# Two copies of F, not one, ahead of the layernorm's last step in layer 0 of a two-layer graph attention kernel

## The chip, the cores and the metric

The kernel runs on one core of one Trainium2 chip. The metric is the time of one execution on the device in microseconds (us); lower is better. A core has five engines that run their own instruction queues side by side and wait for each other by semaphores: TensorE (PE in the profile), VectorE (DVE), ScalarE (ACT), GpSimd (POOL) and SyncE (SP). In this kernel POOL issues the gathers and scatters and SP the plain transfers.

## The reference, cut to what matters

Two graph attention layers run on 2708 nodes with 1024 features. The adjacency matrix is sparse and symmetric with a full diagonal; a node has about 17 neighbours.

```python
def _layernorm(x, axis=-1, eps=1e-5):
    m = jnp.mean(x, axis=axis, keepdims=True)
    v = jnp.var(x, axis=axis, keepdims=True)
    return (x - m) / jnp.sqrt(v + eps)

# layer 0
f = x @ Wf + bf
g = x @ Wg + bg
e = jax.nn.relu(f @ g.T)
scores = jnp.where(adj > 0, e, NEG)
attention = jax.nn.softmax(scores, axis=1)
x = _layernorm(x + attention @ (x @ W + bW))

# layer 1
h = x @ W
e = leaky_relu(h @ a1 + (h @ a2).T)
attention = softmax(where(adj > 0, e, NEG), axis=1)
x = _layernorm(x + relu(attention @ h))
```

## The kernel before, in words

A prelude turns the adjacency matrix into a list of neighbours for each node and folds Wf and Wg into one matrix M, so that the score of a node and a neighbour is a dot product of the node's row of F = x M with the neighbour's row of x (plus terms that depend on one of the two alone). The nodes are sorted by their number of neighbours and cut into 22 blocks of 128 (one has 32).

A block of 128 nodes has four groups of 32. A group's 32 nodes stand four times in the 128 partitions, so that one gathered tile of 128 rows holds four neighbours of each of the 32 nodes. A block has some 15 to 20 such tiles. They lie in `ring`, a buffer of 20 tiles in SBUF.

For a group, the 32 rows of F that belong to it have to stand four times below each other, too. That is what `replicate` does: four copies by ScalarE of 32 x 1024 numbers each, from the PSUM tile of F (`pm`) into an SBUF tile `Fr`. There are four `Fr` buffers, one for each group of a block. The scores are then made by `dots`: for each gathered tile one VectorE instruction multiplies the tile with its group's `Fr` and sums along the row (tile `j` is the product nobody reads). The tiles are taken in the order group 0, group 1, group 0, group 1 and so on, and then groups 2 and 3 in the same way.

The loop of layer 0 (line 1242) is a pipeline over blocks. Iteration k does, by engine:

- **VectorE**: the residual sum `z` and the layernorm's statistics of block k-1 (`close` and `norm`; the last of its small steps is `sh`), the query product of a later block (`q_dot`, `j<-xb,rb`), two products of the finished z with vectors that layer 1 needs (`j<-z,u2b` and `j<-z,u1b`), a reciprocal, the score products of block k+1 (`dots`), and their softmax (`soft`), which ends with `st`, the weights as TensorE wants them.
- **ScalarE**: copies of transposed y, group 0 of F of block k+1, the layernorm's last step (`z<-z,sh,rstd`, which waits for `sh` from VectorE), groups 1 and 2 of F, the scaling of block k's result (`y<-po,ri`), two copies of transposed x, group 3 of F, and later the exponential of the softmax.
- **TensorE**: the weighted sums of block k (`po<-ring,st`, which need `st`), transposes of x of block k+2, the product with W for block k-1, the product with M for block k+2 (the next F), transposes of y of block k.
- **GpSimd**: the gathers of block k+1's tiles, each as soon as the sums of block k have freed its place in the ring, then the scatter of z into layer 1's table (`T<-z`), and the loads of x, of the residual z and of later lists.
- **SyncE**: the write of z to memory (`X1S<-z`), behind the layernorm's last step.

Each engine keeps the order in which the program is written: the class `InOrder` (its line 71 is the line that the profile shows for every instruction of these layers, so instructions are told apart by their tiles). `close` is a generator: its first `next` runs the sum and the statistics up to `sh`, the second the layernorm's last step on ScalarE and SyncE's write, the third the two products on z, and what is left the scatter. So the place of a `replicate` between the `next(closing)` lines is its place in ScalarE's queue.

Of the kernel before, what the change touches and what calls it, by code (L numbers as in the profile page):

```python
# [106 lines left out]
def listed_path(ctx, tc, x, adj, Wf, bf, Wg, bg, W, bW, W1, a1, a2, out):  # L107
# [96 lines left out]
    def u_rows():  # L204

        for v, u in enumerate((u1b, u2b)):
            for h in range(H):
                pt = ps_t.tile([P, 4, P], F32, name="pt")
                for c in range(4):
                    k = 4 * h + c  # L210
                    pe.matmul(pt[:, c, :], uc[:, v, k:k + 1].to_broadcast([P, P]), ident, start=True, stop=True)
                act.copy(u[:, h * 512:(h + 1) * 512], pt.rearrange("p c i -> p (c i)"))
# [506 lines left out]
    def turn(rows, n, dst, halves=False):  # L719


        pts = []
        for k0 in range(0, KC, 4):
            pt = ps_t.tile([P, 4, P], F32, name="pt")
            at = slice(64, 64 + n) if halves and k0 and n < P else slice(0, n)
            for k in range(4):
                pe.transpose(pt[:, k, :n], rows[at, (k0 + k) * P:(k0 + k + 1) * P], ident[at, at])
            pts.append(pt)
        yield
        for k0, pt in zip(range(0, KC, 4), pts):  # L730
            if halves and k0 and n == P:
                for a, b in ((0, 64), (64, 0)):
                    act.copy(dst[:, k0:k0 + 4, a:a + 64], pt[:, :, b:b + 64])
            else:
                act.copy(dst[:, k0:k0 + 4, :n], pt[:, :, :n])

    def product(n, xT, w, row=None):


        pm = ps_m.tile([P, H, 512], F32, name="pm")  # L740
        for h in range(H):
            bias_row(pm, h, n, row)
        for h in range(H):
            half_product(pm, h, n, xT, w, row)
        return pm
# [20 lines left out]
    def split_product(xT, w, parts, row=None, pm=None):  # L766

        pm = ps_m.tile([P, H, 512], F32, name="pm") if pm is None else pm  # L770
        for h in range(H):
            c = slice(h * 512, (h + 1) * 512)
            if row is not None:
                pe.matmul(pm[:32, h, :], pick[:, row:row + 1].to_broadcast([P, 32]), rows3[:, c], start=True, stop=False)
            for k in range(KC // Q):
                for p in range(Q):
                    i = p * KC // Q + k
                    pe.matmul(pm[32 * p:32 * p + 32, h, :], xT[:, i, :32], w[:, i, c],
                              start=(k == 0 and (row is None or p > 0)), stop=(k + 1 == KC // Q))
        yield  # L780
        act.copy(parts, flat(pm))
        yield
        pm = ps_m.tile([P, H, 512], F32, name="pm")
        for h in range(H):
            pe.matmul(pm[:, h, :], rep, parts[:, h * 512:(h + 1) * 512], start=True, stop=True)
        return pm

    def whole(steps):

        while True:  # L790
            try:
                next(steps)
            except StopIteration as end:
                return end.value
# [261 lines left out]
    def load_lists(b):  # L1056
        for g in groups[b]:
            gather(pool, SL[:, g, :], LD[:, :], idq[:, g:g + 1], N * Q)
# [9 lines left out]
    with s0s:  # L1068
# [9 lines left out]
        def load_x(b):  # L1078
            xb[b] = xp.tile([P, D], F32, name="xb") if b > 0 else zs[:, :D]
            gather(pool, xb[b][:nrows[b]], x, ids[:nrows[b], b:b + 1])  # L1080
# [5 lines left out]
        def q_dot(b):  # L1086
            n = nrows[b]
            qs = small.tile([P, 1], F32, name="qs")
            dot(xb[b][:n], rb, n, qs[:n])
            qd[b] = spread(qs[:n], n, "qd")  # L1090

        def q_spread(b):
            n = nrows[b]
            pt = ps_t.tile([P, 4, P], F32, name="pt")
            pe.matmul(pt[:, 0, :Q], rep[:n], qd.pop(b)[:n], start=True, stop=True)
            yield
            q[b] = small.tile([P, Q], F32, name="q")
            dve.tensor_scalar(q[b], pt[:, 0, :Q], s0, None, op0=ALU.add)

        def x_turn(b):  # L1100
            xTs[b] = tp.tile([P, KC, P], F32, name="xT")
            for _ in turn(xb[b], nrows[b], xTs[b]):
                pass

        def f_product(b):
            F[b] = product(nrows[b], xTs.pop(b), M, 0)

        def replicate(b, k):

            Fr[b, k] = frp.tile([P, D], F32, name="Fr")  # L1110
            for p in range(Q):
                act.copy(Fr[b, k][32 * p:32 * p + 32, :], flat(F[b])[32 * k:32 * k + 32, :])

        def dots(u, lo, hi):
            for m in range(lo, hi):
                k, g, t = u.tiles[m]
                dot(lay.rows(u.at + m), Fr[u.b, k], P, u.sc[:, k, t:t + 1])
# [6 lines left out]
        def load_residual(b):  # L1124

            t, at = lay.slots[(lay.next + b + 2 - NB) % lay.count]
            Z[b] = zs if b + 2 < NB else t[:, at, :]
            gather(pool, Z[b][:nrows[b], :D], x, ids[:nrows[b], b:b + 1])
# [113 lines left out]
        for k, u in enumerate(units):  # L1242
            nxt = units[k + 1] if k + 1 < len(units) else None
            b = u.b
            back = seq[k - 1] if k > 0 else None
            ahead = seq[k + 2] if k + 2 < NB else None

            first = k == 0
            po = ps_s.tile([P, H, 512], F32, name="po")
            y[b] = yp.tile([P, D], F32, name="y")  # L1250
            if back is not None:
                for _ in yTs[back][1]:
                    pass
            reps = list(range(len(nxt.gs))) if nxt is not None and not first else []
            for r in reps[:1]:
                replicate(nxt.b, r)
            next(closing, None)
            if loaded is not None:
                q_dot(loaded)
                loaded = None  # L1260
            next(closing, None)
            for r in reps[1:3]:
                replicate(nxt.b, r)
            if nxt is None:

                for _ in closing:
                    pass
                Wp[back] = product(P, yTs.pop(back)[0], Wt, 1)
            lay.sums(u, po, y[b])
            if first:  # L1270
                u_rows()
            for _ in closing:
                pass
            closing = iter(())
            if ahead is not None and not first:
                x_turn(ahead)
            if k + 3 < NB and not first:
                loaded = seq[k + 3]
                load_x(loaded)
            if back is not None and nxt is not None:  # L1280
                load_residual(back)
                if back > 0:
                    Wp[back] = product(P, yTs.pop(back)[0], Wt, 1)
                else:
                    Wp[back] = whole(split_product(yTs.pop(back)[0], Wt, frp.tile([P, D], F32, name="Fr"), 1))
            if k + 2 == NB:
                load_residual(b)
            spreading = iter(())
            if ahead is not None and not first:
                spreading = q_spread(ahead)  # L1290
                next(spreading)
            for r in reps[3:]:
                replicate(nxt.b, r)
            if ahead is not None and not first:
                f_product(ahead)
            if ahead == NB - 1:
                sp.dma_start(M, W1.rearrange("(k p) d -> p k d", p=P))
            yT = tp.tile([P, KC, P], F32, name="xT")
            steps = turn(y[b], nrows[b], yT, halves=True)
            next(steps)  # L1300
            yTs[b] = yT, steps
            if k + 2 == NB:
                for _ in steps:
                    pass
            if k + 4 < NB and not first:
                load_lists(seq[k + 4])
            if nxt is not None:
                dots(nxt, 0, len(nxt.tiles))
            for _ in spreading:
                pass  # L1310
            if nxt is not None:
                soft(nxt)
            if back is not None:
                closing = close(back)
                next(closing)
# [529 lines left out]
```

## Time and profile before

| | us |
|---|---|
| median of 3 runs | 1885.37 |
| lowest and highest of them | 1868.06, 1900.10 |
| the profiled execution's own time | 1889.49 |
| its span, first to last instruction | 1887.8 |

| engine | busy us in the span | share | busy us from 507 to 1020 us |
|---|---|---|---|
| PE | 1614.6 | 86% | 489.55 |
| DVE | 1279.9 | 68% | 442.15 |
| ACT | 637.6 | 34% | 248.53 |
| POOL | 1180.3 | 63% | 362.23 |

The stretch from 507 to 1020 us holds twelve blocks of layer 0's loop. The mean of one 32 x 1024 copy of F is close to 1.0 us, that of one score product 1.23 us.

The profile is that of one execution. A row of groups gives busy time and the mean of one instruction, a row of waits gives the engine, the tile that it was about to write, what ended the wait, then the total in us, how often, and the longest. In a timeline the bracket is the engine's idle time ahead of the instruction and what ended it; "issue" means that the profile shows nothing that it waited for. Where a wait has several causes, the last by the profile is named.

### The profile page before, as it was taken

How to read it: one execution, taken by the hardware profiler on the slowest of the kernel's cores; microseconds unless marked ns; L12 is line 12 of the kernel's file. 1: busy time of each engine (PE TensorE's matmuls, PEld its weight loads, DVE VectorE, ACT ScalarE, POOL GpSimd, SP SyncE). 2: the span in 40 equal slices, each digit the busy share in tenths (PEclk: the TensorE clock that was granted, in tenths of full speed). 3: DMA queues.
4: the chain of work that ended last, by engine and by line, in shares of the span. 5: the costliest groups of instructions: out<-in, count | busy, mean ns of one | idle time of the engine just before them, and what ended most of it. 6: DMA issues, size and time to landing. Idle time of an engine off the chain costs nothing. (4 is left out here: it accounts for less than half of the span.)

```text
span 1887.8 us, 22782 instructions
## 1 busy us (share of the span) xinstructions
PE 1614.6 (86%) x6873; PEld 684.2 (36%) x6873; DVE 1279.9 (68%) x4158; ACT 637.6 (34%) x886; POOL 1180.3 (63%) x1130
## 2 busy tenths in 40 slices
PE   3898759788999999999999998279898988989896
PEld 2443324333443444444444443023333333323332
DVE  5996648767888888888888767246445445545543
ACT  5571425434554544444555551011111111111111
POOL 8892673555676777766767631666666666666630
PEclk7999889888999999999999999589999999989998
DMA  9671583656787778887777863999989999999950
GB/s 365 227 284 50 193 293 116 223 176 238 284 278 270 277 251 274 280 281 262 262 257 263 310 239 136 342 329 320 321 319 348 351 347 317 343 333 352 341 190 35
DMA packets 150961, 503.95 MB, mean 267 GB/s; under 512 B 32714, under 2 KB 32730, under 8 KB 148398
## 3 DMA queue, kind: packets, MB, share of 16 engines
q0 software_dynamic: 131648, 428.27, 63.9%
q1 hardware_dynamic: 16128, 73.71, 10.5%
q8 instruction: 56, 0.92, 0.2%
q10 hardware_dynamic: 3054, 0.43, 0.1%
q14 instruction: 75, 0.61, 0.1%
HBM read 510.81 MB, written 33.75 MB: 288 GB/s over the span
## 5 line engine op out<-in xcount | busy, mean ns | idle before, releaser
L71 POOL DMA_INDIRECT ring<-in_x_dram,SL x405 | 447.2, 1104 | 210.7 <-issue 95.1
L71 DVE SCALAR_TENSOR_TENSOR j<-ring,Fr 128x1024 bf16<-128x1024 f32 x402 | 493.1, 1227 | 100.3 <-ACT Fr L71 41.9
L71 PE MATMUL po<-ring,st 128*32 128x512 f32 x2616 | 376.9, 629 | 109.9 <-issue 56.2
L71 ACT COPY Fr<-pm 32x1024 f32<-32x1024 f32 (+2 forms) x353 | 340.6, 965 | 15.1 <-remote 6.5
L71 POOL DMA_INDIRECT ring<-T,SL x249 | 246.9, 992 | 122.9 <-issue 64.5
L71 PE MATMUL pm<-M,yT 128*128 128x512 f32 (+1 forms) x704 | 318.2, 601 | 4.5 <-issue 3.0
L71 PE MATMUL pm<-Wt,xT 128*128 128x512 f32 (+1 forms) x704 | 305.8, 603 | 12.2 <-issue 12.2
L71 PE MATMUL pm<-M,xT 128*128 128x512 f32 x672 | 298.5, 603 | 2.4 <-issue 2.4
L71 PEld LDWEIGHTS po<-ring,st 128*32 128x32 f32 x2616 | 109.4, 115 | 322.3 <-issue 258.6
L71 POOL DMA_INDIRECT more<-T,SL x156 | 155.0, 993 | 76.9 <-issue 42.8
L71 PEld LDWEIGHTS pm<-M,yT 128*128 128x128 f32 (+1 forms) x704 | 127.7, 187 | 195.7 <-issue 192.9
L71 PEld LDWEIGHTS pm<-Wt,xT 128*128 128x128 f32 (+1 forms) x704 | 131.2, 189 | 175.0 <-issue 171.1
L71 ACT ACTIVATE scores<-scores 128x12 f32<-128x12 f32 (+9 forms) x65 | 14.0, 216 | 520.2 <-DVE scores L71 415.2
L71 PEld LDWEIGHTS pm<-M,xT 128*128 128x128 f32 x672 | 130.5, 194 | 160.9 <-issue 158.2
L71 POOL TENSOR_TENSOR adj<-adj,iota 128x2708 f32<-128x2708 f32 (+2 forms) x23 | 124.5, 5446 | 17.0 <-ACT adj L71 17.0
L71 ACT ACTIVATE y<-po,ri 128x512 f32<-128x512 f32 (+1 forms) x88 | 58.1, 684 | 211.7 <-remote 134.4
L71 PE MATMUL pm<-halfT,Wt 128*128 128x512 f32 x256 | 114.3, 602 | 0.0
L71 POOL DMA_INDIRECT SL<-LD,idq x85 | 88.4, 1040 | 28.4 <-issue 25.8
L71 PE MATMUL po<-more,st 128*32 128x512 f32 x624 | 94.0, 659 | 13.2 <-issue 13.1
L71 DVE MAX8 cand<-adj 128x8 f32<-128x170 f32 x336 | 95.9, 325 | 12.4 <-POOL adj L71 12.4
L71 ACT COPY xT<-pt 128x512 f32<-128x512 f32 (+2 forms) x109 | 47.9, 499 | 85.6 <-PE pt L71 56.7
L71 POOL DMA_INDIRECT z<-in_x_dram,ids x21 | 25.1, 1194 | 81.3 <-DVE j L71 26.3
(236 smaller groups left out, 1436.0 us busy)
## 6 DMA issues: line engine op xcount, KB each, us to landing
adj<-in_adj_dram SPq DMA_DIRECT2D x19, 1354.0 KB
X1S<-z SPq DMA_DIRECT2D x19, 512.0 KB
ring<-in_x_dram,SL POOLq DMA_INDIRECT x405
rows<-in_L_gnn_Wg_dram SPq DMA_DIRECT2D x8, 512.0 KB
rows<-in_L_gnn_Wf_dram SPq DMA_DIRECT2D x8, 512.0 KB
M<-in_L_gnn_W_dram SPq DMA_DIRECT2D x1, 4096.0 KB
ring<-T,SL POOLq DMA_INDIRECT x249
u1b<-X1S SPq DMA_DIRECT2D x7, 512.0 KB
```

The source lines that it names most:

```text
L71: made = self.tc.keep_in_program_order(op(*args, **kwargs))
```

## The change

In each iteration of layer 0's loop, ScalarE's copies of group 1 of the next block's F move ahead of the layernorm's last step of the block before. Group 0 stands there already; group 2 stays behind it, and group 3 stays where it is. No instruction is added or taken away.

```diff
@@ -1252,14 +1252,14 @@
                 for _ in yTs[back][1]:
                     pass
             reps = list(range(len(nxt.gs))) if nxt is not None and not first else []
-            for r in reps[:1]:
+            for r in reps[:2]:
                 replicate(nxt.b, r)
             next(closing, None)
             if loaded is not None:
                 q_dot(loaded)
                 loaded = None
             next(closing, None)
-            for r in reps[1:3]:
+            for r in reps[2:3]:
                 replicate(nxt.b, r)
             if nxt is None:
```

## The prediction

> **What bounds the kernel now.** I began with the page's slices, because the change touches layer 0 alone and a share over the whole span says nothing of it.
>
> ```profile
> PE   3898759788999999999999998279898988989896
> DVE  5996648767888888888888767246445445545543
> ACT  5571425434554544444555551011111111111111
> PEclk7999889888999999999999999589999999989998
> ```
>
> A slice is 1887.8 / 40 = 47.2 us. Layer 0's loop runs from about 300 to 1150 us, slices 7 to 24. There TensorE (PE) is near full, from slice 10 on at its full clock, VectorE (DVE) at eight tenths and ScalarE (ACT) at four to five tenths. ACT has room; the question is whom its order keeps waiting. Next I asked who waits for whom in a stretch of twelve like blocks, 507 to 1020 us (43 us each), first for DVE (three of its rows), then for ACT, then for PE:
>
> ```profile
> DVE j L71 <- DMA ring<-in_x_dram,SL: 27.3, 49, 1.8
> DVE j L71 <- issue: 6.4, 13, 2.0
> ...
> DVE j L71 <- ACT Fr L71: 2.4, 8, 0.3
> ```
>
> ```profile
> ACT z L71 <- DVE sh L71: 32.4, 12, 5.6
> ```
>
> ```profile
> PE po L71 <- DVE st L71: 14.3, 11, 2.5
> PE po L71 <- issue: 7.6, 16, 0.8
> ```
>
> So PE waits for DVE's softmax weights (st) in eleven of twelve blocks, 1.3 us each: here a block ends when DVE ends. But DVE itself waits in its score products (j), some 3 us a block, mostly until a gathered row has landed in the ring. ACT, ahead of z, waits for DVE's sh.
>
> Third, the timeline of one block, ACT first. Columns are start, duration, instruction, number; the bracket is the idle time before it:
>
> ```profile
> 856.19 4.04 ACT L71 COPY Fr<-pm 32x1024 f32<-32x1024 f32 x4
> 862.34 1.24 ACT L71 ACTIVATE z<-z,sh,rstd 128x1024 f32<-128x1024 f32 x1 [2.11 <-DVE sh L71]
> 863.61 8.13 ACT L71 COPY Fr<-pm 32x1024 f32<-32x1024 f32 x8
> 871.76 1.27 ACT L71 ACTIVATE y<-po,ri 128x512 f32<-128x512 f32 x2
> ```
>
> One group of F is copied, ACT idles 2.11 us until the layernorm's shift is there, scales z, and copies two groups in one run. The same block on DVE:
>
> ```profile
> 862.09 0.22 DVE L71 TENSOR_SCALAR sh<-mv,rstd 128x1 f32<-128x1 f32 x1
> 862.21 1.22 DVE L71 SCALAR_TENSOR_TENSOR j<-xb,rb 128x1024 bf16<-128x1024 f32 x1
> ...
> 863.61 1.23 DVE L71 SCALAR_TENSOR_TENSOR j<-z,u2b 128x1024 bf16<-128x1024 f32 x1
> ...
> 866.15 1.23 DVE L71 SCALAR_TENSOR_TENSOR j<-ring,Fr 128x1024 bf16<-128x1024 f32 x1
> ...
> 867.69 1.23 DVE L71 SCALAR_TENSOR_TENSOR j<-ring,Fr 128x1024 bf16<-128x1024 f32 x1 [0.30 <-issue]
> ...
> 869.67 1.23 DVE L71 SCALAR_TENSOR_TENSOR j<-ring,Fr 128x1024 bf16<-128x1024 f32 x1 [0.75 <-DMA ring<-in_x_dram,SL]
> ...
> 889.51 1.23 DVE L71 SCALAR_TENSOR_TENSOR j<-ring,Fr 128x1024 bf16<-128x1024 f32 x1 [0.59 <-DMA ring<-in_x_dram,SL]
> ```
>
> The query product (j from xb) hides ACT's 1.24 us on z exactly: z's first product starts at 863.61 without a wait. Two products on z follow, then the score products; the second needs the second F group, and ACT's run delivers that at 863.61 + 4.06 = 867.67: DVE waits 0.30. That 0.30 is the price of today's order, and it is in nearly every block. Later score products wait for rows, the last at 889.51.
>
> **The change, part by part.** Nothing is added or removed. In 19 blocks (z starting between 321 and 1119 us) four 32x1024 copies, 4.06 us, pass ahead of z's scaling on ACT; the other engines' orders and POOL's and SP's issue orders stay as they are.
>
> *z's scaling, later.* ACT has the second group's F and a free Fr buffer (its last reader is the softmaxed block before), so the copies fill ACT's idle time and z starts 4.06 minus that idle later: 4.06 - 2.11 = 1.95 us in the block above. Behind z on DVE stand its two products (1.23 each), the reciprocal, and all score products: DVE idles those 1.95 us, from 863.6 to 865.55.
>
> *Second F group, earlier.* It is ready before the first score product, so the 0.30 goes. Net 1.65 us late from the second score product on.
>
> *What is late next.* Each later score product starts when its row has landed or when DVE is free. The rows' gathers follow PE's sums on POOL, started by the previous st, not by these products; I take the landings as fixed. A product that waited now waits that much less, and the delay shrinks by each wait. In this block the waits after the second product add to 0.75 + 0.48 + 0.40 + 0.19 + 0.31 + 0.29 + 0.59 = 3.0 us, more than 1.65: st stays where it is. The same replay in every block (ACT's idle before z; delay of z; DVE's waits over 0.12 us after the second product; what is left at st):
>
> | z starts (us) | idle | delay | waits | left |
> |---|---|---|---|---|
> | 321, 371, 423 | 0 | 4.06 | 4.1, 7.4, 7.9 | 0 |
> | 472 | 0 | 4.06 | 1.46 | 2.29 |
> | 515, 557, 646, 690, 733, 776 | 2.94, 2.08, 2.53, 2.95, 2.29, 2.82 | 1.1 to 2.0 | 3.2, 3.3, 3.0, 3.3, 3.2, 2.4 | 0 |
> | 604 | 5.6 | 0 | 2.4 | 0 |
> | 819, 862, 905, 948, 990 | 2.03, 2.11, 2.92, 2.04, 2.07 | 1.1 to 2.0 | 4.0, 3.0, 3.2, 2.5, 2.4 | 0 |
> | 1032 | 2.09 | 1.97 | 1.16 | 0.51 |
> | 1074 | 2.56 | 1.50 | 7.6 | 0 |
> | 1119 | 0 | 4.06 | 1.26 | 2.50 |
>
> The last 0.51 and 2.50 are hidden: PE takes up those blocks' st 3.5 us and more after it is made (st at 1062.5 and 1146.3, PE's sums at 1066.9 and 1150.7). The 2.29 at 472 is not: PE waited 0.17 us for that st. **Sum: +2.3 us.** If the cover were gone everywhere, see the first rival.
>
> *ACT's later work.* With its idle filled, ACT ends the third group, the scaling of y and the fourth group up to 2 us sooner. Nobody waits: PE runs from the x transposes at 867.28 to the end of the F product at 896.8 without a gap, and y's transposes stand behind that. I cost it at nothing; at most it gives the idle filled, 31 us over thirteen blocks.
>
> *SP's write of z and POOL's scatter.* The write is issued right behind z's scaling, 2 us later, and first reports come 2.5 us on; the scatter of z stands behind the block's gathers on POOL (888.60 here), 20 us later. Nothing.
>
> [...]
>
> **The total.** Profiled execution: span 1887.8 plus 1.7 around it = 1889.5; after, 1891.8. That execution is 4.1 us above the median of the three runs, 1885.4, so I give 1885.4 + 2.3 = **1888 us**.
>
> **Rivals.**
>
> *Slower: the delay reaches the matmuls.* Price: 5 blocks x 4.06 + 13 x 4.06 - 31.4 (idle of those thirteen) - 18 x 0.30 = 36.2 us; 1925.7 against the profile, 1921.6 against the median, +1.9%. For it: DVE releases PE in most blocks, and the margin is thin in some (1.7 against 2.4 at 990). Against it: the rows' landings are what DVE last waits for, and the three early blocks and 1074 have over 7 us or PE behind them. It decides once a block's waits for rows are below z's delay less 0.30, about 1.7 us, or if rows land later along with the products. Half exposed is 1904.
>
> *Faster: the copies are what counts.* DVE loses 18 x 0.30 = 5.4 us and nothing is given back: 1880 by the median. If ACT's gained idle also shortened blocks, 31 us: 1854. For it: ACT's idle is real. Against: z is waited for first by the same DVE, and PE's floor without any wait in the twelve blocks is (14.3 + 7.6) / 12 = 1.8 us a block below today, so 31 is out of reach.
>
> *No change at all*, because the order isn't what the diff says, is excluded: in the compiled order ACT's z stands behind four more copies in 19 blocks.
>
> **How the numbers follow.** Forecast 0.74, slower rival 0.17, faster rival 0.09. The three runs lie 17 us below to 15 above their median, and about 2% (38 us) is what a measurement tells from no change. The range goes from the faster rival's 1880 less half that spread, 1872, to the full exposure, 1921. Over 2% slower needs more than the full price, or that and a slow draw: half of that rival, rounded up, 0.10; over 2% faster has no mechanism, 0.03; within 0.87.
>
> **What would show it.** ACT's wait for sh ahead of z gone; the products on z waiting for ACT z about 1 to 2 us in each block of 507 to 1020; the 0.30 for the second F group gone; DVE's waits for rows down by some 1.5 us a block; PE's waits for st about as before (14 us) and blocks of 43 us. Wrong would be: waits for rows as large as before with longer blocks (the slower rival: landings move with DVE), or blocks shorter with PE waiting less for st.

## The result and the profile after

| | before | changed |
|---|---|---|
| median of 6 runs, us | 1888.92 | 1942.16 |
| lowest to highest | 1868.06 to 1900.10 | 1929.21 to 1952.61 |
| profiled execution, its span | 1889.49, 1887.8 | 1946.41, 1944.7 |

The ratio is 1.0295, 95% interval 1.0258 to 1.0331: slower, 53 us, where the forecast had 1888 and the range ended at 1921.

The page's slices of the changed kernel (those of before stand in the prediction):

```profile
PE   3896858898988898989999889359988888988876
DVE  5996648787878786868888667336445464544533
ACT  5571443544343444444445354001111111111111
PEclk8998879898989899989999899679989999989988
```

Every layer-0 engine is less busy, and PE's clock is no longer full in the middle. The loop, from the first to the last scaling of z, took 832.5 us before and 876.9 now: 44 of the 57 us that the spans differ by. Of the rest, 5 us lie ahead of the first of these scalings, 4.06 of them the copies that now stand in front of it, and 7 us behind the last, where no instruction was moved.

The waits of 507 to 1020 us, first DVE (its rows on `j`), then PE (all its rows on `pt`, and the one between them):

```profile
DVE j L71 <- issue: 51.3, 9, 8.9
DVE j L71 <- ACT Fr L71: 22.0, 3, 9.6
DVE j L71 <- ACT z L71: 11.0, 3, 4.6
```

```profile
PE pt L71 <- DVE ri L71: 16.5, 5, 3.3
PE pm L71 <- issue: 14.7, 14, 2.2
PE pt L71 <- issue: 13.2, 4, 3.3
PE pt L71 <- DVE j L71: 6.7, 2, 3.4
```

Two rows of before are gone: DVE waits for no row of the ring any more (27.3 us), and PE does not wait for st (14.3 us). In their place DVE waits for z, eleven times and 59 us in all (the row `ACT z` and 48 us of the first row, by the timeline), and PE waits eleven times, 3.3 us each, before it writes a tile `pt`. That tile is the one that PE's transposes go to. The profile names DVE's reciprocal `ri` for five of these waits, the product beside it for two and nothing for four; in time each ends as the one below does, with the reciprocal. One block of the changed kernel, ACT, DVE and PE in turn:

```profile
931.90 1.14 ACT L71 COPY xT<-pt 128x512 f32<-128x512 f32 x3 [2.84 <-PE pt L71]
932.91 8.12 ACT L71 COPY Fr<-pm 32x1024 f32<-32x1024 f32 x8
941.06 1.24 ACT L71 ACTIVATE z<-z,sh,rstd 128x1024 f32<-128x1024 f32 x1
942.33 4.06 ACT L71 COPY Fr<-pm 32x1024 f32<-32x1024 f32 x4
```

```profile
942.34 1.23 DVE L71 SCALAR_TENSOR_TENSOR j<-z,u2b 128x1024 bf16<-128x1024 f32 x1 [5.18 <-issue]
943.60 1.23 DVE L71 SCALAR_TENSOR_TENSOR j<-z,u1b 128x1024 bf16<-128x1024 f32 x1
...
944.75 0.17 DVE L71 RECIPROCAL ri<-pt 128x2 f32<-128x2 f32 x1
```

```profile
941.03 0.66 PE L71 MATMUL pt<-ident,xb 128*128 128x128 f32 x4
944.97 0.66 PE L71 MATMUL pt<-ident,xb 128*128 128x128 f32 x4 [3.29 <-DVE j L71]
...
945.90 15.59 PE L71 MATMUL pm<-Wt,xT 128*128 128x512 f32 x32
...
961.90 13.89 PE L71 MATMUL pm<-M,xT 128*128 128x512 f32 x32
975.63 1.04 PE L71 MATMUL pt<-ident,y 128*128 128x128 f32 x8
```

The same places on PE and DVE in the kernel before:

```profile
867.28 1.10 PE L71 MATMUL pt<-ident,xb 128*128 128x128 f32 x8
...
868.65 13.90 PE L71 MATMUL pm<-Wt,xT 128*128 128x512 f32 x32
```

```profile
866.03 0.17 DVE L71 RECIPROCAL ri<-pt 128x2 f32<-128x2 f32 x1
```

There are two `pt` buffers. In `sums` PE writes the softmax's totals into one, and only the reciprocal frees it. The second half of the x transposes needs that buffer. Before, the reciprocal was done at 866.20 us and the second half due at 867.7: some 1.5 us to spare. In the changed kernel the late z holds z's two products, they hold the reciprocal, and PE stands still in the middle of its transposes.

That closes a ring of waits, with its own length, in this block and the next: x transposes and the two products of PE 30.66 us (944.97 to 975.63), to the copies of y's transposes 0.69, two of those 1.01, eight copies of F 8.15, z's scaling 1.27, two products and the reciprocal 2.59, back to PE 0.05: **44.42 us**. In the list of z's starts eight of the nineteen intervals are 44.4 us and one 44.2, seven are 48 to 53, and ACT has no idle time ahead of z in any but the last. One more thing is in it: the product with W takes 15.59 us, not 13.90. The trace's windows of the kernel, with the granted clock as the third number from the end, show why:

```profile
946.00:949.40 3.40, 3.40 (x6) 1.32 (x5) 3.30 (x7) 3.35 (x6) 2.79 (x3) 0.50 1.02 406
949.40:990.00 40.60, 37.31 (x177) 16.20 (x177) 33.55 (x77) 17.02 (x21) 24.40 (x25) 1.00 0.73 249
```

The hole ends at 944.97 us; from 946.00 to 949.40 us PE is granted half its clock (0.50), then 1.00, and the product with W takes 1.7 us more than the 13.90 us of before.

The seven long intervals are not explained by this. The kernel before has three such, 49 to 52 us, all before 475 us. In all of them but the first of either kernel ACT stands still for 2 to 8 us at a time ahead of y's scaling or the copies of transposed x, and the profile names no instruction of this core that it waits for ("remote" or "issue"). So here, at 843 to 897 us of the changed kernel:

```profile
853.59 1.27 ACT L71 ACTIVATE y<-po,ri 128x512 f32<-128x512 f32 x2 [5.00 <-issue]
...
866.28 0.59 ACT L71 COPY xT<-pt 128x512 f32<-128x512 f32 x1 [7.12 <-remote]
```

In the same six of the seven PE, too, pauses 1.0 to 2.2 us at a time within or behind the product with W, and a second stretch at 0.50 of the clock, of 3.4 to 10.2 us, goes with them. By the intervals, the nine of 44.2 to 44.4 us are 1.4 us each over the 43.0 of before, some 13 of the 44 us; most of the rest stands in the four long intervals more. So on this chip the ring is shown, but what it is worth there is not.

### The profile page after: what moved, and what is told of

Its sections match the earlier page's. It is cut to its first block, busy times and chain, and to the rows that moved or that the text cites. A ratio compares the mean times of both kernels' runs of the same rounds, so it can differ in the third digit from the quotient of the medians.

```text
span 1944.7 us, 22760 instructions
## 1 busy us (share of the span) xinstructions
PE 1616.7 (83%) x6851; PEld 682.5 (35%) x6873; DVE 1281.3 (66%) x4158; ACT 638.6 (33%) x886; POOL 1151.4 (59%) x1130
## 5 line engine op out<-in xcount | busy, mean ns | idle before, releaser
L71 POOL DMA_INDIRECT ring<-in_x_dram,SL x405 | 418.0, 1032 | 276.9 <-issue 82.2
L71 PE MATMUL po<-ring,st 128*32 128x512 f32 x2616 | 342.5, 619 | 85.7 <-issue 34.1
L71 PE MATMUL pm<-Wt,xT 128*128 128x512 f32 (+1 forms) x704 | 333.1, 645 | 18.7 <-issue 18.5
L71 PEld LDWEIGHTS pm<-Wt,xT 128*128 128x128 f32 (+1 forms) x704 | 141.5, 204 | 198.2 <-issue 194.3
L71 PEld LDWEIGHTS po<-ring,st 128*32 128x32 f32 x2616 | 96.1, 113 | 276.5 <-issue 218.6
L71 DVE SCALAR_TENSOR_TENSOR j<-z,u2b 128x1024 bf16<-128x1024 f32 (+1 forms) x20 | 24.6, 1228 | 118.6 <-issue 84.8
```

Of the source, the lines that this page charges most:

```text
L71: made = self.tc.keep_in_program_order(op(*args, **kwargs))
```

## The experiments

Theory A is the one above: PE waits for the reciprocal, which stands behind the products on z. Its numbers for the ring, by subtraction from 44.42: less the half clock 1.70, less the 4.06 of copies that the change put into it, the kernel before has a ring of 38.7 us, well under its blocks of 43. Theory B is the first rival of the forecast: DVE's own wait for z reaches st. Theory C is a part of A: the hole brings the half clock (in the changed kernel's trace sixteen of the seventeen holes at the x transposes, 3.2 to 5.0 us, go with one of 3.4 us or more), and that keeps the ring above 43.

The runs came to two sorts of chip: in medians, the kernel before took 1732 to 1735 us on one and 1879 to 1889 on the other. The clock that PE was granted over the whole execution of the kernel before was 0.953 to 0.961 on one and 0.932 to 0.950 on the other. A ratio is always to the kernel before on the same chip.

**The reciprocal ahead of the products on z, in the changed kernel.** The two products now run where the rest of `close` runs, after `sums`.

```diff
             if loaded is not None:
                 q_dot(loaded)
                 loaded = None
-            next(closing, None)
             for r in reps[2:3]:
```

> The changed kernel, with the two products on z moved behind the reciprocal on VectorE (the copies of group 1 stay ahead of z's scaling). Theory A (the transposes of x wait on TensorE for the buffer that the reciprocal reads, and the reciprocal stands behind the products on z): the 3.3 us holes of TensorE ahead of the second half of the x transposes go, blocks return to about 43 us, time 1880 to 1900 against 1889 of before. Theory B (the late z delays VectorE itself up to st, wherever the reciprocal stands): VectorE waits as long for z, blocks stay at 44 us and more, time 1930 to 1950.

1742.24 us, 1.0072 (1.0056 to 1.0089), on a quick chip. The holes at the x transposes are gone from the loop, blocks are 41.7 us. What is left shows in its waits from 500 to 1000 us, PE and DVE:

```profile
PE po L71 <- DVE st L71: 23.8, 12, 2.7
```

```profile
DVE j L71 <- ACT z L71: 25.7, 12, 2.3
```

DVE waits 2.1 us for z in each of twelve blocks, and PE for st. So A is the bulk of the loss, and B is real but small. On this chip DVE waits for no row there (in the kernel before on the first chip 26.2 us in the same stretch), so there is nothing that could absorb z's delay. Two more runs, one meant for a chip with late rows, came to the quick sort as well:

> The changed kernel with the two products on z behind the reciprocal, again, for a chip on which the rows land late. The first run of it was on a quick chip (1.007 of before), where VectorE's wait of 2.0 us for z reached st. On a slow chip the waits for rows absorb it: 0.99 to 1.003 of before. On a quick chip again 1.007. If rows don't absorb it: 1.007 and more on either.

1744.52 us, 1.0060 (1.0045 to 1.0075).

> The changed kernel with the reciprocal ahead of the products on z, for a slow chip (before at about 1885 us). There the forecast's step is tested by itself: rows land late, DVE's waits for rows in the kernel before are some 3 us a block, so they absorb z's delay of 2 us: 0.99 to 1.003 of before, and VectorE's waits for rows are down to about 1 us a block. If the landings move with the products: 1.007 or more. On a quick chip 1.006 once more, and the step stays untested.

1744.14 us, 1.0074 (1.0051 to 1.0097). The forecast's step that late rows absorb z's delay has not been tried by itself: no run of this kernel came to a slow chip.

**The same in the kernel before.**

> The kernel before, with the two products on z moved behind the reciprocal on VectorE. Theory A: the steady blocks had 1.1 us to spare there, so nothing changes in them; the blocks from 321 to 472 us and at 1074 us, where ScalarE is late and TensorE had holes at the x transposes, get shorter: time 1865 to 1889. Theory B: the products on z only change places with work of the same engine: 1885 to 1893.

1725.61 us, 0.9971 (0.9953 to 0.9990). The ring of the steady blocks, 38.7 us by the subtraction above, is under their length already, so there is little to win. No difference at all is outside the interval, but the lower end of what B had, 1885 of 1889, is not, so this does not decide between the two theories, nor do its repeats below. (The expectation was wrong about the early holes: in the profile before the x transposes of 321 to 472 us run without one, and only those at 1074 us have it.) Repeated, and once more:

> The kernel before with the two products on z behind the reciprocal, again, on what chip comes. Theory A: on a quick chip 0.997 as in the first run; on a slow chip the holes of the blocks from 321 to 472 us and at 1074 us go, too: 0.985 to 1.0.

1729.15 us, 0.9974 (0.9963 to 0.9986).

> The kernel before with the reciprocal ahead of the products on z. On a slow chip the holes at the x transposes of the blocks at 321 to 472 us and 1074 us go: 0.985 to 1.0. On a quick chip 0.997 as twice measured.

1728.78 us, 0.9977 (0.9965 to 0.9989). All three are on quick chips: a version a quarter of a per cent faster than the kernel before. It also gives the right partner for the three runs above. On each chip the changed kernel with the reciprocal ahead is 15 to 17 us slower than the kernel before with the reciprocal ahead (1742.24 and 1725.61, 1744.52 and 1729.15, 1744.14 and 1728.78): that is the price of the moved copies once nobody waits for the reciprocal.

**Half of the delay.** Two of group 1's four copies ahead of z (`replicate` now takes the range of copies).

```diff
...
             for r in reps[:1]:
                 replicate(nxt.b, r)
+            for r in reps[1:2]:
+                replicate(nxt.b, r, 0, 2)
             next(closing, None)
...
-            for r in reps[1:3]:
+            for r in reps[1:2]:
+                replicate(nxt.b, r, 2, Q)
+            for r in reps[2:3]:
                 replicate(nxt.b, r)
```

> Two of group 1's four copies ahead of z's scaling, two behind it. Theory A: the ring of waits (z, its products, reciprocal, x transposes, the two products of TensorE, y's transposes, copies, z) takes 44.42 us in the changed kernel; with 2.03 us less ScalarE work in it 42.4, which is under the 43.0 us of the kernel before, so the loss is gone, or nearly: 1885 to 1905. Theory B: the loss goes with the delay of z, half of 53 us: 1910 to 1920.

1735.29 us, 1.0025 (1.0007 to 1.0042). B's half of the loss is not there. Thirteen of the nineteen intervals are 40.7 us: 38.7 + 2.03 = 40.7. From 500 to 1000 us PE waits twelve times for the reciprocal, once 3.7 us and the other times 1.2 us in the mean, and is granted 0.99 of its clock. (The 42.4 of the expectation still had the half clock in it.) In these runs a ring about as long as the blocks of some 40.5 us cost next to nothing (40.7 us: 0.25%), and a longer one about what it is longer in each of 18 blocks (further down, 42.7 us: 33 us; 44.4 us: 61 us).

**The reciprocal late, with the copies as before.** No copy and no scaling is moved; in the kernel before the reciprocal goes behind the first four score products.

```diff
+            if ahead is not None:
+                ahead()
             ri = small.tile([P, H], F32, name="ri")
...
-            lay.sums(u, po, y[b])
+            early = 4 if nxt is not None and not first else 0
+            lay.sums(u, po, y[b], lambda: dots(nxt, 0, early) if early else None)
...
-                dots(nxt, 0, len(nxt.tiles))
+                dots(nxt, early, len(nxt.tiles))
```

> The kernel before, with the reciprocal moved behind the first four score products on VectorE; the copies of F and z's scaling stay as before, no engine has more to do. Theory A: the ring of waits is 44.42 less 4.06 (no copies of group 1 ahead of z) less 1.70 (half clock) = 38.7 us in the kernel before; four score products of 1.27 us make it 43.7, with the half clock 45.4: TensorE has holes of 3 us and more at the x transposes, and the time is 1.01 to 1.03 of before on a slow chip (its blocks are 43), 1.03 to 1.05 on a quick one (blocks of 40). Theory B (VectorE's own delay is what counts): no engine is delayed by this, 0.998 to 1.003.

1841.32 us, 1.0619 (1.0603 to 1.0635): twice the loss of the change, from a 0.17 us instruction that only changed its place on one engine. Blocks are 45 to 47.5 us. PE's only wait from 500 to 1000 us:

```profile
PE pt L71 <- DVE ri L71: 55.0, 11, 5.5
```

More than expected, because the four products bring their own waits for rows and for group 1 into the ring (some 1 us a block), and PE is slower behind the holes, which are 5.0 us in the mean: behind those of 4.97 and 5.45 us the second half of the transposes takes 1.12 and 1.11 us (0.66 in the changed kernel's block above) and the product with W 14.39 and 15.18 us (13.90 before). The clock granted over the whole execution is 0.930 to 0.933, that of the kernel before on this chip 0.954 to 0.960.

**Only a delay.** The kernel before copies group 0 twice ahead of z (the second time over the first); group 1 stays behind z.

```diff
             for r in reps[:1]:
                 replicate(nxt.b, r)
+                for p in range(Q):
+                    act.copy(Fr[nxt.b, r][32 * p:32 * p + 32, :], flat(F[nxt.b])[32 * r:32 * r + 32, :])
             next(closing, None)
```

> The kernel before with group 0 of F copied twice ahead of z's scaling; groups 1 and 2 stay behind it. ScalarE has 4.06 us more to do in each block, group 1 is not earlier. Theory A: only the length of the ring counts, so it is as slow as the changed kernel, within 1%. If instead the early place of group 1 did the harm: near the kernel before, under 1.01 of it.

1937.54 us, 1.0321 (1.0127 to 1.0515), with the changed kernel beside it on the same slow chip:

> The changed kernel once more, beside the others, since the chip of the first four runs was quicker than the first one (before 1732 us there, 1889 on the first). Theory A with C: the ring of waits does not depend on the rows' landings and is 44.4 us with the half clock; against blocks of 40.5 us of the kernel before on a quick chip this is 4 us in some 18 blocks, so 1.03 to 1.045 of before. Theory B: rows land in time on a quick chip, nothing absorbs z's delay of 2 us, 36 us: 1.02.

1951.04 us, 1.0463 (1.0330 to 1.0596). The two are within 1%, with a spread of 14 to 37 us in each, and both have holes of 3.2 to 3.4 us from the second block on (the last 5.0). So it does not matter that it is group 1 that stands ahead of z, only that 4.06 us of work do.

**The hole filled.** Two more matmuls per block, just ahead of the second half of the x transposes; they go into the PSUM tile of the product with W, which overwrites them.

```diff
...
         for k0 in range(0, KC, 4):
+            if fill is not None and k0:
+                for _ in range(2):
+                    pe.matmul(fill[:, 0, :], ident, Wt[:, 0, :512], start=True, stop=True)
             pt = ps_t.tile([P, 4, P], F32, name="pt")
```

> The changed kernel with two more matmuls (128x128 by 128x512, 0.87 us each, result overwritten) in each of 18 blocks on TensorE, just ahead of the second half of the x transposes. Theory C, as a part of A (a hole of over 3 us on TensorE is followed by 3.4 us at half the clock, 1.7 us lost in each block, and that keeps the ring of waits long): the holes shrink to under 2 us, the half clock goes from most blocks, time falls by 15 to 40 us from the 1942 of the changed kernel though there is more work. If the half clock has nothing to do with the holes: no gain, 1935 to 1975 (the added 18 x 1.74 us are 31).

1765.47 us, 1.0207 (1.0190 to 1.0224), on a quick chip without the changed kernel beside it; so again beside it, on a slow chip:

> The changed kernel with two more matmuls ahead of the second half of the x transposes, as before, now on one chip with the changed kernel itself. Theory C: blocks of 42.7 us instead of 44.4, 25 to 35 us less than the changed kernel, though with 31 us more of matmuls. Without C: the changed kernel's time or more.

1914.45 us, 1.0249 (1.0106 to 1.0392): 37 us less than the changed kernel's 1951.04, with 31 us more of matmuls. Eleven of its intervals are 42.7 us, just under the first chip's 43.0 of before, and yet it is 36 us above the kernel before on its own chip; its trace has five long intervals of 50 to 60 us, that of the changed kernel beside it nine of 48 to 60. No trace of the kernel before was taken there, so what these are worth stays open. On the quick chips no interval is over 47.5 us.

**The parts on one chip.** Last, the changed kernel, the holes filled and the reciprocal ahead on one (quick) chip.

> The changed kernel on one chip with the next two kernels. On a quick chip (before at about 1732 us, blocks of 40.5): blocks of 44.4 us with holes of 3.3 us, 1.035 to 1.045 of before. On a slow one: 1.03 to 1.05, as twice measured.

> The changed kernel with two more matmuls in each hole. Blocks of 42.7 us on either chip, between the two others: 1.02 on a quick chip, 1.01 to 1.025 on a slow one; the changed kernel less this is the share of the half clock, 1.7 us a block.

> The changed kernel with the reciprocal ahead of the products on z. On a quick chip 1.006 to 1.007, as twice measured: what is left when the holes are gone, VectorE's own wait for z. On a slow chip the waits for rows absorb that: 0.985 to 1.003.

| kernel | us | ratio to before (95%) | blocks, us |
|---|---|---|---|
| before | 1733.90 | 1 | about 40.5 (no trace on such a chip; an estimate from the kernel with only the reciprocal ahead, 39.6 to 41.6 in most blocks) |
| changed, reciprocal ahead | 1743.23 | 1.0056 (1.0036 to 1.0077) | 41.7 |
| changed, hole filled | 1767.14 | 1.0198 (1.0176 to 1.0221) | 42.7 |
| changed | 1795.21 | 1.0360 (1.0339 to 1.0381) | 44.4 |

Of the 61 us, 28 are the half clock behind the hole, by the difference of the last two rows (PE was granted 0.96 of its clock from 500 to 1000 us in the changed kernel, 1.00 with the hole filled), 24 the ring without it, and 9 what is left when the reciprocal is ahead, where DVE's wait for z reaches st. The 9 are a net figure: the reciprocal ahead wins 4 to 6 us by itself, so z's delay by that path is worth the 15 to 17 us of above. The hole in the changed kernel and what the filling makes of it:

```profile
669.53 0.66 PE L71 MATMUL pt<-ident,xb 128*128 128x128 f32 x4 [3.27 <-DVE ri L71]
...
670.64 15.40 PE L71 MATMUL pm<-Wt,xT 128*128 128x512 f32 x32
```

```profile
655.55 1.88 PE L71 MATMUL pm<-Wt,ident 128*128 128x512 f32 x4
658.98 0.66 PE L71 MATMUL pt<-ident,xb 128*128 128x128 f32 x4 [1.55 <-DVE ri L71]
...
659.90 13.90 PE L71 MATMUL pm<-Wt,xT 128*128 128x512 f32 x32
```

Behind the hole of 3.27 us PE is granted 0.54 of its clock from 670.0 to 673.4 us, and the product with W takes 15.40 us; behind the hole of 1.55 us it takes 13.90.

**A try for a better version: the products on z in the middle of the score products**, behind groups 0 and 1, so that neither the reciprocal nor the first score products wait for z. The rest of `close` and the loads behind it move with them.

```diff
...
-            next(closing, None)
             for r in reps[2:3]:
                 replicate(nxt.b, r)
...
-            for _ in closing:
-                pass
-            closing = iter(())
             if ahead is not None and not first:
                 x_turn(ahead)
...
+            if nxt is not None:
+                dots(nxt, 0, half)
+            for _ in closing:
+                pass
+            closing = iter(())
+            if back is not None and nxt is not None:
+                load_residual(back)
...
-                dots(nxt, 0, len(nxt.tiles))
+                dots(nxt, half, len(nxt.tiles))
```

> The changed kernel with the two products on z moved behind the reciprocal and behind the score products of groups 0 and 1 on VectorE (z's scatter and the next residual's load follow them on GpSimd). Theory A and B together: neither the reciprocal nor the score products stand behind the late z any more, so nothing waits for z: 0.985 to 1.0 of before. If what is left of the loss in the kernel with the reciprocal ahead (1.007 of before) was not VectorE's wait for z: 1.005 to 1.01 again.

1891.95 us, 1.0131 (0.9970 to 1.0293), on a slow chip: unclear, no gain. The holes at the x transposes are gone, all but one of 4.0 us, yet DVE now waits for rows twice as long as in the kernel before (26.2 us there, from 500 to 1000 us, on the first chip):

```profile
DVE j L71 <- DMA ring<-in_x_dram,SL: 54.2, 43, 3.2
```

Why it does was not shown. An estimate that no run tests: in the kernel before the two products on z take 2.54 us of DVE in a block (863.61 to 866.15 us), ahead of the first score product; here they no longer fill that time, and at 43 us a block that is 30 us from 500 to 1000 us, near the 28.0 us by which the waits for rows grew (54.2 less 26.2).

## Why the prediction was wrong

- **The step that failed** is under "z's scaling, later". It lists what stands behind z on DVE, the reciprocal among it, and then follows the score products alone. Nobody was asked for who waits for the reciprocal. "ACT's later work ... Nobody waits: PE runs from the x transposes ... without a gap" was true of the profile, and no measure of how much later the reciprocal might come: the spare was 1.5 us, less than z's delay of up to 2. What the runs showed in its place is a hole of 3.3 us on PE in each block, and with the half clock behind it 52 of the 61 us on a quick chip.
- **The second failure follows from it**: "z starts 4.06 minus that idle later". One hole makes PE late, PE makes y's transposes late, they make ACT late, and ACT's idle time, which was to take up 2 us of the copies, is gone. The delay was taken per block with the next block's starting point unchanged; in a ring it isn't. The view before had shown both halves: blocks from 321 to 472 us with no idle time ahead of z, and a hole of 3.46 us at the x transposes that ends at 1078 us. I read them as cover, not as warnings.
- **The half clock** wasn't in the forecast at all. It is 28 of 61 us on a quick chip. Without it the ring is 42.7 us, just under the blocks of 43.0 of the kernel before on the first chip. The changed kernel's trace on the first chip has one such block: from 800.54 to 843.27 us, 42.7 us, with a hole of 3.29 us and a clock of 1.00 behind it.
- **The slower rival** had the sign and the range's upper side, but another path and price. Its path, DVE's wait reaching st, costs 15 to 17 us where the two kernels differ by the copies alone and the reciprocal is ahead in both, not 36.2: there DVE waited some 2 us for z in each block, but only part of it passed to the end. That was on quick chips, where no late rows take it up.
- **What held**: the 0.30 us for the second F group is gone (the 22.0 us on `Fr` after the change are three waits of 4 to 10 us for a later group, each in a long interval); DVE's waits for rows shrank (to nothing); the write of z and the scatter cost nothing that shows. ACT's wait for sh ahead of z is gone, too. The sign "products on z waiting for ACT z" came, with 5.2 us in the blocks of 44.4 us in place of 1 to 2. "PE's waits for st about as before" did not: they are gone, since in those blocks st is now made 2.1 to 2.3 us ahead of its use.

## What to carry to other kernels

When a step is moved back, ask for every instruction queued behind it what it frees as well as what it makes: here a 0.17 us instruction that releases a PSUM buffer held TensorE for 3.3 us a block, and for some 5 us when it was put later still. If the waits close a ring over several engines, add up its length and compare it with the block: here a delay that left the ring about as long as the block was nearly free (2.03 us cost 0.25%), and one that made it longer was paid in every block, and idle time of one engine in the ring isn't a reserve that can be spent twice. And keep the instruction that frees a scarce buffer ahead of whatever may wait.

## What the runs showed that was not expected

Not every hole went with a half clock on TensorE. In the changed kernel on the first chip there are seventeen holes at the x transposes, 3.2 to 5.0 us. With sixteen of them the granted clock is 0.50 for 3.4 us or more, beginning between 1.4 us ahead of the hole's end and 1.1 us behind it. With the one of 3.29 us that ends at 804.46 us it is 1.00 up to 846.9 us, and the product with W takes 13.90 us. On one quick chip the changed kernel had eleven holes from 500 to 1000 us, 3.3 us each, at a mean clock of 0.96; with the holes filled there were eleven of 1.6 us, at 1.00. In the kernel before on the first chip PE waited up to 2.5 us for st eleven times from 507 to 1020 us and was granted 1.00 of the clock throughout. In the changed kernel with the reciprocal ahead (first run) it waited for st twelve times from 500 to 1000 us, up to 2.7 us, at a mean clock of 0.99; behind the wait of 2.25 us that ends at 679.68 us the first sixteen sums took 2.86 us, behind that of 0.81 us in the next block 1.92. So in these runs the length of a hole alone does not tell whether a half clock goes with it.

Adding 31 us of matmuls made a kernel 28 to 37 us faster. And the same kernel took 1732 us on some chips and 1885 on others. In the changed kernel on the first chip, one of the slow sort, the clock was also 0.50 in other places than behind these holes, in the long intervals above (632.0 to 638.7 us and 864.1 to 874.3 us, for two). Why it was so was not found.
